# RWKV stage of a four-stage network: from strings of a whole sequence to strings of one chunk

## The chip, the cores and the metric

The kernel runs on one core of a Trainium2 chip. The metric is the device time of one execution in microseconds (us). Three runs of the kernel before gave 1712.28, 1715.19 and 1717.48 us; the median is 1715.19 us.

The core has a matrix engine (PE; its weight loads are shown apart as PEld), a vector engine (DVE), an activation engine (ACT), a general engine (POOL) and a queue that issues transfers (SP). Each works through its own queue in order; they wait for each other by semaphores.

## The reference

Four stages work on an input of 4 sequences, 1024 tokens and 128 channels: an RWKV block, a mixture of experts with grouped routing, a linear attention with decay, and a causal attention with a second mixture of experts. Only the first is touched. Its time mixing, cut to what matters:

```python
def step(carry, kv):              # over the tokens
    aa, bb = carry
    kk, vv = kv
    p = jnp.maximum(bb, u + kk)
    e1 = jnp.exp(bb - p)
    e2 = jnp.exp(u + kk - p)
    out = (e1 * aa + e2 * vv) / (e1 + e2)
    p2 = jnp.maximum(bb, kk)
    e1b = jnp.exp(bb - p2)
    e2b = jnp.exp(kk - p2)
    return ((e1b * aa + e2b * vv, p2 + jnp.log(e1b + e2b)), out)
```

Around it stand a layer norm, a shift by one token, three projections (k, v, r) and a sigmoid gate. Channel mixing follows on the sum: a layer norm, a shift by one token that takes its first token from the end of the sequence, a projection to 512 channels with a squared relu, one back to 128, and a gate.

## The kernel before

The activations stay on the chip with the channels on the 128 partitions and the tokens along the free dimension. A sequence of 1024 tokens is two chunks of 512 (`CH`, `NH`); an instruction of the stage works on 128x512 float32 numbers. The recurrence over the tokens is three scans of the vector engine per chunk: a running maximum (`mx`, L262), a running sum (`ss`, L273) and the weighted values (`aa`, L289). What a scan leaves at the end of chunk 0 is copied into `carry` (`keep`, L211) and read at the start of chunk 1 (`chained`, L206).

The stages are called A (RWKV), B (experts), C (linear attention) and the attention loop. A, B and stage C of sequences 0 and 1 are placed on the engines by the tile framework's scheduler, which goes by program order as a priority and by what is ready, and so lets stages overlap. The attention loop behind them is written out by hand, with stage C of sequences 2 and 3 inside it.

Stage A is a generator (`stage_a`, L186). A sequence is one string of work: time mixing of chunk 0 (L221 to L311), time mixing of chunk 1, then channel mixing of both (L315 to L346). Each `yield` ends a step; a loop (L721 to L730) takes one step of every running sequence per round. It holds at most three sequences (`SIDE = 3`) and starts a new one when twelve rounds have passed since the last start (`BEHIND = 12`) and fewer than three run:

```python
if waiting and (len(running) == 0 or (len(running) < SIDE and count >= BEHIND)):
    b = waiting.pop(0)
    running.append(stage_a(b, rooms_a[b % SIDE]))
    count = 0
running = [g for g in running if not next(g, True)]
```

Buffers go by sequence: `own` is `_0`, `_1` or `_2`, and under it there is one each of the nine chunk buffers `hs`, `xxx`, `k`, `v`, `r`, `mx`, `d`, `ss` and `aa`, one each of `x1` and `h2` (a whole sequence), and two of the scratch `rs` (`Room.scratch`, L111). So the two chunks of a sequence share one set. All three sequences take their matmul results from three PSUM banks (`pp_a`), with time mixing and channel mixing on the same three. Two more banks (`pp_c`) belong to stage C and later stages, three (`pp_b`) to stage B.

The lines that the prediction goes by: L227 to L234 load, centre and transpose a chunk (`x_t`); L242 to L252 the norm and the token shift (`xxx`); L255 the projection to `k`; L310 the last instruction of a chunk's time mixing (`h`); L345 the last of a chunk's channel mixing (it adds to `xT`). In stage B, L463 opens each of a sequence's 18 units (9 groups of experts in each of two halves), L482 and L483 close a half. In stage C, L526 is the first instruction of a half. Stage C's buffer pool `pc` is opened on the left side of the on-chip memory, where `pa`, the pool of stage A, has been closed just before.

Of the kernel before, what the change touches and what calls it, by code (L numbers as in the profile page):

```python
# [18 lines left out]
P = 128  # L19
NB = 4  # L20
# [19 lines left out]
def sandwich(ctx: ExitStack, tc: tile.TileContext, x, vecs, cmats, rope, wa, wb, wc, wd, out):  # L40
# [61 lines left out]
    class Room:  # L102


        def __init__(self, pool, stage, bufs, sbuf=None, own=""):
            self.pool, self.stage, self.bufs, self.sbuf, self.own = pool, stage, bufs, sbuf, own
# [4 lines left out]
        def scratch(self, tag, shape=(P, CH), bufs=2):  # L111
            return self.sbuf.tile(list(shape), FP, tag=tag + self.own, name=tag, bufs=bufs)
# [73 lines left out]
    def stage_a(b, pp):  # L186

        own = pp.own
        ts = vec("time_shift")

        def buf(tag, shape=(P, CH), bufs=1):
            return pa.tile(list(shape), FP, tag=tag + own, name=tag, bufs=bufs)

        x1 = buf("x1", (P, T))
        h2 = buf("h2", (P, T + 1))

        carry = buf("carry", (P, 4), 2)
        nc.gpsimd.tensor_copy(carry[:, 0:1], ts)
        nc.gpsimd.memset(carry[:, 1:2], 0.0)
        nc.gpsimd.memset(carry[:, 2:3], 1.0)  # L200
        nc.gpsimd.memset(carry[:, 3:4], 0.0)

        def chained(tag, which):

            t = buf(tag, (P, CH + 1))
            nc.gpsimd.tensor_copy(t[:, 0:1], carry[:, which : which + 1])  # L206
            return t

        def keep(t, which, h):
            if h + 1 < NH:  # L210
                nc.gpsimd.tensor_copy(carry[:, which : which + 1], t[:, CH : CH + 1])  # L211

        def sigmoid_steps(dst, src, plus=0.0):
            nc.vector.tensor_scalar(dst, src, plus, -41.0, ALU.add, ALU.max)
            yield
            nc.scalar.activation(dst, dst, AF.Exp, scale=-1.0)
            nc.scalar.activation(dst, dst, AF.Ln, bias=one)
            nc.scalar.activation(dst, dst, AF.Exp, scale=-1.0)
            yield

        for h in range(NH):  # L221
            c = chunk(h)
            if (b, h) not in xtok:
                load_x(b, h)
            xt = xtok[b, h]
            at = means[:, b, h * 4 : h * 4 + 4]
            nc.vector.tensor_reduce(at, xt, AX.X, ALU.add)  # L227
            nc.vector.tensor_scalar_mul(at, at, 1.0 / P)
            nc.gpsimd.tensor_sub(xt, xt, at.unsqueeze(2).to_broadcast([P, 4, P]))
            yield  # L230
            pt = pp([P, CH], "x_t")
            for j in range(4):
                nc.tensor.transpose(pt[:, j * P : (j + 1) * P], xt[:, j, :], ident)
            nc.scalar.copy(xT[b][:, c], pt)  # L234
            yield

            var = mean_square(pp, xT[b][:, c])
            yield
            rs = rstd(var, eps5, to=pp.scratch("rs"))
            both = rstd(var, eps10, scale=1.0 + 1e-5)  # L240
            yield
            nc.gpsimd.tensor_mul(x1[:, c], xT[b][:, c], rs)  # L242
            hs = chained("hs", 0)
            nc.vector.scalar_tensor_tensor(
                hs[:, 1:], xT[b][:, c], vec("ln1_w"), both, op0=ALU.mult, op1=ALU.mult
            )
            nc.vector.tensor_scalar_add(hs[:, 1:], hs[:, 1:], vec("ln1_b"))
            keep(hs, 0, h)
            yield
            xxx = buf("xxx")  # L250
            nc.gpsimd.tensor_sub(xxx, hs[:, 1:], hs[:, :CH])
            nc.vector.scalar_tensor_tensor(xxx, xxx, ts, hs[:, 1:], op0=ALU.mult, op1=ALU.add)  # L252
            yield
            k, v, r = buf("k"), buf("v"), buf("r")
            nc.scalar.copy(k, project(pp, wat[:, 0, :], xxx, "k_ps"))  # L255
            nc.vector.tensor_copy(v, project(pp, wat[:, 1, :], xxx, "v_ps"))
            yield
            later_r = sigmoid_steps(r, project(pp, wat[:, 2, :], xxx, "r_ps"))


            mx = chained("mx", 1)
            nc.vector.tensor_tensor_scan(mx[:, 1:], k, k, mx[:, 0:1], op0=ALU.max, op1=ALU.max)  # L262
            keep(mx, 1, h)
            yield
            next(later_r)
            d = buf("d")
            nc.gpsimd.tensor_sub(d, mx[:, :CH], mx[:, 1:])
            nc.scalar.activation(d, d, AF.Exp)
            ss = chained("ss", 2)
            nc.gpsimd.tensor_sub(ss[:, 1:], k, mx[:, 1:])  # L270
            nc.scalar.activation(ss[:, 1:], ss[:, 1:], AF.Exp)
            yield
            nc.vector.tensor_tensor_scan(ss[:, 1:], d, ss[:, 1:], ss[:, 0:1], op0=ALU.mult, op1=ALU.add)  # L273
            keep(ss, 2, h)
            yield from later_r
            nc.scalar.activation(d, ss[:, :CH], AF.Ln)
            yield
            nc.vector.tensor_add(d, d, mx[:, :CH])
            nc.vector.tensor_sub(d, d, k)
            yield  # L280
            e1, e2 = mx[:, :CH], k
            nc.vector.tensor_scalar_min(e1, d, 0.0)
            nc.scalar.activation(e1, e1, AF.Exp)
            nc.vector.tensor_scalar_max(e2, d, 0.0)
            nc.scalar.activation(e2, e2, AF.Exp, scale=-1.0)
            yield
            nc.vector.tensor_mul(e2, e2, v)
            aa = chained("aa", 3)
            nc.vector.tensor_tensor_scan(aa[:, 1:], e1, e2, aa[:, 0:1], op0=ALU.mult, op1=ALU.add)  # L289
            keep(aa, 3, h)  # L290
            yield

            yield from sigmoid_steps(d, d, nfirst)
            o = xxx
            nc.gpsimd.tensor_sub(o, aa[:, :CH], v)
            nc.vector.tensor_mul(o, o, d)
            yield
            nc.gpsimd.tensor_add(o, o, v)
            nc.vector.tensor_mul(o, o, r)
            yield  # L300
            nc.gpsimd.tensor_add(x1[:, c], x1[:, c], o)
            yield
            pc_ = project(pp, center, x1[:, c], "ln_c")
            var = mean_square(pp, pc_)
            yield
            rs = rstd(var, eps5, to=pp.scratch("rs"))
            yield
            now = h2[:, 1 + h * CH : 1 + (h + 1) * CH]
            nc.vector.scalar_tensor_tensor(now, pc_, vec("ln2_w"), rs, op0=ALU.mult, op1=ALU.mult)
            nc.vector.tensor_scalar_add(now, now, vec("ln2_b"))  # L310
            yield  # L311


        nc.gpsimd.tensor_copy(h2[:, 0:1], h2[:, T : T + 1])
        for h in range(NH):  # L315
            c = chunk(h)
            now = h2[:, 1 + h * CH : 1 + (h + 1) * CH]
            xx2 = buf("xxx")
            nc.gpsimd.tensor_sub(xx2, h2[:, c], now)
            nc.vector.scalar_tensor_tensor(xx2, xx2, ts, now, op0=ALU.mult, op1=ALU.add)  # L320
            yield
            rc = buf("r")
            later_r = sigmoid_steps(rc, project(pp, wat[:, 11, :], xx2, "rc_ps"))
            next(later_r)
            kcs = []
            for j in range(4):
                kc = pa.tile([P, CH], FP, tag="kc", name="kc", bufs=4)
                nc.scalar.activation(kc, project(pp, wat[:, 3 + j, :], xx2, "kc_ps"), AF.Relu)
                nc.scalar.activation(kc, kc, AF.Square)
                kcs.append(kc)  # L330
            pv = pp([P, CH], "vv_ps")
            for j in range(4):
                nc.tensor.matmul(pv, lhsT=wat[:, 7 + j, :], rhs=kcs[j], start=(j == 0), stop=(j == 3))
            yield
            yield from later_r
            nc.vector.tensor_mul(rc, pv, rc)
            nc.gpsimd.tensor_add(rc, rc, x1[:, c])
            yield
            pc_ = project(pp, center, rc, "ln_c")
            var = mean_square(pp, pc_)  # L340
            yield
            rs = rstd(var, eps5, to=pp.scratch("rs"))
            yield
            nc.vector.tensor_mul(rc, pc_, rs)
            nc.gpsimd.tensor_add(xT[b][:, c], xT[b][:, c], rc)  # L345
            yield  # L346
# [372 lines left out]
    rooms_a = [Room(pp_a, "a", 3, pa, f"_{i}") for i in range(SIDE)]  # L719
    room_b = Room(pp_b, "b", 3, pb)  # L720

    running, waiting = [], list(range(NB))
    count = 0
    while running or waiting:
        if waiting and (len(running) == 0 or (len(running) < SIDE and count >= BEHIND)):
# [553 lines left out]
```

## Time and profile before

| what | value |
|---|---|
| median of three runs | 1715.19 us |
| the profiled execution | 1715.55 us, its span 1713.8 us |
| instructions in the span | 15167 |
| granted PE clock, mean | 0.85 |
| L234, copy of a transposed chunk (8 of them) | 8.5 to 239.0 us |
| L310, end of time mixing (8 of them) | 59.0 to 279.8 us |
| L345, end of channel mixing (8 of them) | 142.9 to 317.9 us |
| L463, opening of an expert unit (72 of them) | 204.5 to 697.1 us |
| L882, first kind of work of the attention loop | from 735.3 us |

The profile is one execution. Times are from the start of its span. A row of instructions gives line, engine, operation, "what it writes <- what it reads", and either start and length in us (the timeline) or the number, the mean and the idle time ahead (the groups). What stands in brackets is the time for which the engine was idle before it, and who released it.

### The profile page before, as it was taken

The page shows a single profiled execution, that of the slowest core. Times are in us where ns is not written, and L with a number is a line of the kernel's source. Part 1 is how long each engine was busy: PE and PEld are TensorE (multiplying, and loading weights), DVE is VectorE, ACT ScalarE, POOL GpSimd, SP SyncE. Part 2 cuts the span into 40 slices and gives each one's busy share as a digit, 9 for nine tenths or more (in the row PEclk, how much of TensorE's full clock was granted, in tenths as well). Part 3 has the DMA queues.
Part 4 walks back from the last instruction along what each step waited for, and adds up shares of the span by engine and source line. Part 5 has one row for each costly group of instructions (what it writes and reads, how often), then busy time and mean ns, then how long its engine had stood idle before and what let it go on. Part 6 is the DMA issues. An engine that isn't in the chain of part 4 may idle for free.

```text
span 1713.8 us, 15167 instructions
## 1 busy us (share of the span) xinstructions
PE 1310.6 (76%) x4593; PEld 463.3 (27%) x4604; DVE 1168.9 (68%) x1991; ACT 856.7 (50%) x1565; POOL 655.9 (38%) x663
## 2 busy tenths in 40 slices
PE   2547887867865889678779869888887879889864
PEld 1213333312221323133223223322232223233311
DVE  4575676698775877867995597777779825577601
ACT  3457776624453457234436625645553345645561
POOL 5554353524252324323433363427227333122212
PEclk8669998978887999877779869987898669989996
DMA  2000110313033122101112111231113011110101
GB/s 97 13 7 6 25 50 25 96 40 108 13 111 110 53 65 85 44 12 34 45 58 70 53 57 54 70 92 46 38 37 101 21 48 64 45 61 29 54 22 56
DMA packets 59330, 90.49 MB, mean 53 GB/s; under 512 B 9904, under 2 KB 26800, under 8 KB 58544
## 3 DMA queue, kind: packets, MB, share of 16 engines
q1 hardware_dynamic: 59248, 89.52, 17.3%
q8 instruction: 36, 0.59, 0.1%
q14 instruction: 46, 0.38, 0.1%
HBM read 76.38 MB, written 12.71 MB: 52 GB/s over the span
## 4 chain that ended last, share of the span: by engine, by line
PE 32%; DVE 18%; ACT 6%; issue 4%; POOL 4%; DMA 2%; SPq 0%; POOLq 0%; DVEq 0%; ACTq 0%
PE av L937 8%; PE sc L945 5%; DVE ms L882 4%; DVE st L620 4%; ACT pr L950 3%; PE sm L874 3%; DVE ms L887 3%; PE y L1074 3%; PE sm L886 2%; PE ln_v L138 2%; PE num_ps L674 1%; POOL hid L473 1%; POOL share L1062 1%; PE sm L878 1%; PE g_ps L138 1%
## 5 line engine op out<-in xcount | busy, mean ns | idle before, releaser
L950 ACT ACTIVATE pr<-sc 128x512 f32<-128x512 f32 x576 | 328.2, 595 | 361.7 <-PE sc L945 358.0
L882 DVE TENSOR_REDUCE ms<-sm 128x1 f32<-128x512 f32 (+3 forms) x352 | 210.5, 633 | 114.2 <-PE sm L878 103.0
L945 PE MATMUL sc<-qr,keys_r 75*128 75x512 bf16 x576 | 234.1, 422 | 37.7 <-ACT pr L950 28.7
L887 DVE TENSOR_REDUCE ms<-sm 128x1 f32<-128x512 f32 x256 | 165.0, 682 | 56.4 <-PE sm L886 55.9
L937 PE MATMUL av<-pr,va 128*32 128x512 f32 x1152 | 183.1, 710 | 0.0
L954 POOL TENSOR_SCALAR_AFFINE_SELECT pr<-pr 128x512 f32<-128x512 f32 x128 | 89.4, 712 | 244.5 <-ACT pr L950 236.2
L874 PE MATMUL sm<-keys_r,qr 72*128 72x512 bf16 (+3 forms) x512 | 138.2, 337 | 46.3 <-DVE ms L882 43.9
L138 PE MATMUL ln_v<-rs,cm 128*128 128x512 f32 x176 | 113.0, 733 | 43.0 <-ACT rs L126 28.3
L473 POOL TENSOR_TENSOR hid<-hid,gate 128x512 f32<-128x512 f32 x64 | 81.9, 1280 | 162.9 <-DVE hid L468 124.6
L614 POOL TENSOR_TENSOR kv<-vrep,phi 128x512 f32<-128x512 f32 x64 | 85.6, 1342 | 115.0 <-issue 47.9
L1062 POOL TENSOR_TENSOR share<-n,every 128x512 f32<-128x512 f32 x64 | 87.2, 1373 | 91.1 <-DMA every<-row 70.5
L455 PE MATMUL y_ps<-hid,wbt 128*128 128x512 f32 x144 | 84.1, 669 | 46.3 <-DVE hid L474 44.4
L886 PE MATMUL sm<-keys_r,qr 72*128 72x512 bf16 x256 | 99.6, 417 | 25.0 <-DVE ms L887 20.6
L945 PEld LDWEIGHTS <-keys_r 75*128 75x128 bf16 x576 | 58.7, 106 | 153.2 <-issue 126.3
L878 PE MATMUL sm<-later,identb 128*128 128x128 bf16 (+2 forms) x341 | 90.5, 265 | 0.0
L474 DVE TENSOR_TENSOR hid<-hid,g 128x512 f32<-128x512 f32 x72 | 57.7, 801 | 46.7 <-POOL hid L473 39.9
L138 PE MATMUL u_ps<-n,wbt 128*128 128x512 f32 x144 | 77.3, 618 | 7.6 <-DVE hid L468 5.1
L138 PE MATMUL g_ps<-n,wbt 128*128 128x512 f32 x144 | 78.8, 630 | 3.7 <-DVE hid L463 1.6
L1074 PE MATMUL y<-share,wexp 128*128 128x512 f32 x128 | 70.8, 644 | 9.6 <-POOL share L1062 9.4
L874 PEld LDWEIGHTS <-qr 72*128 72x128 bf16 x512 | 51.0, 107 | 99.4 <-issue 82.8
L465 ACT ACTIVATE g<-hid 128x512 f32<-128x512 f32 x72 | 45.1, 626 | 55.4 <-DVE hid L463 55.3
L674 PE MATMUL num_ps<-st,cm 128*32 128x512 f32 x128 | 52.5, 777 | 25.7 <-DVE st L637 25.5
(300 smaller groups left out, 2394.9 us busy)
## 6 DMA issues: line engine op xcount, KB each, us to landing
gate<-rows SPq DMA_DIRECT2D x64, 256.0 KB
vrep<-v_rows SPq DMA_DIRECT2D x64, 256.0 KB
every<-row SPq DMA_DIRECT2D x64, 256.0 KB
qr<-dq SPq DMA_DIRECT2D x72, 128.0 KB
turn<-in_rope_dram SPq DMA_DIRECT2D x8, 512.0 KB
dq<-qp SPq DMA_DIRECT2D x8, 384.0 KB
keys_r<-dk SPq DMA_DIRECT2D x72, 32.0 KB
sums<-av_sb SPq DMA_DIRECT2D x128, 18.0 KB
```

Source lines behind the costliest of these rows:

```text
L138: nc.tensor.matmul(ps, lhsT=lhsT, rhs=rhs, start=True, stop=True)
L473: nc.gpsimd.tensor_mul(a, a, gate)
L874: nc.tensor.matmul(view[:, k, :], lhsT=qr[0:KROWS, h, tb], rhs=kr[0:KROWS, half, h // 4, 0:n_s], start=(k == 0), stop=False, skip_group_ch ...
L878: nc.tensor.matmul(view[:, :, n_s - P :], lhsT=identb, rhs=later[:, :in_bank, :], start=False, stop=True, skip_group_check=True,)
L882: nc.vector.tensor_reduce(ms[:, 0, h0 : h0 + in_bank], view, AX.X, ALU.max)
L886: nc.tensor.matmul(sc, lhsT=qr[0:KROWS, h, tb], rhs=kr[0:KROWS, 0, h // 4, :], start=True, stop=True)
L887: nc.vector.tensor_reduce(ms[:, 1, h : h + 1], sc, AX.X, ALU.max)
L937: nc.tensor.matmul(pavs[b, i][32 * g : 32 * g + 32, :], lhsT=va[:, j, g, :], rhs=pr, start=(j == 0), stop=(j == i),)
L945: nc.tensor.matmul(sc, lhsT=kr[0:ROWS, j // 4, g, j % 4 * P : (j % 4 + 1) * P], rhs=qr[0:ROWS, 4 * g : 4 * g + 4, tb], start=True, stop=True,)
L950: nc.scalar.activation(pr, sc, AF.Exp)
L1062: nc.gpsimd.tensor_mul(shares[-1], n4, gates[len(shares) - 1])
L1074: nc.tensor.matmul(y, lhsT=wexp[:, e, :], rhs=shares[e], start=False, stop=(e == 7))
```

## The change

The string of a sequence is cut into strings of a chunk. `time_mixing(b, h, pp)` is the old loop body for one chunk, `channel_mixing(b, h, pp)` the old second loop's body for one chunk; the instructions inside are the same.

- The nine chunk buffers go by chunk: chunk number `2b + h` takes set `(2b + h) % 4` (`SETS = 4`). `x1`, `h2` and `carry` go by sequence, three of each (`SEQS = 3`).
- The loop starts a chunk's time mixing six rounds after the last one's start (`BEHIND = 6`) if fewer than four run; sequence 3 waits until both channel mixings of sequence 0 are done.
- When both chunks of a sequence have had their time mixing, their channel mixings are put into a second list, from which one is started every four rounds (`BEHIND_MIX = 4`).
- Channel mixing takes its matmul results from the two banks of `pp_c`, with its own buffers `xx2` and `rc` (two each) and its own scratch (two). Time mixing keeps the three banks of `pp_a` and has four scratch buffers.
- The load of a chunk's input is issued in the second step of the chunk two places ahead of it, not by the sequence when it gets there.

```diff
-        def scratch(self, tag, shape=(P, CH), bufs=2):
-            return self.sbuf.tile(list(shape), FP, tag=tag + self.own, name=tag, bufs=bufs)
+        def scratch(self, tag, shape=(P, CH)):
+            return self.sbuf.tile(list(shape), FP, tag=tag + self.own, name=tag, bufs=self.kept)
...
-    def stage_a(b, pp):
...
-        x1 = buf("x1", (P, T))
-        h2 = buf("h2", (P, T + 1))
-        carry = buf("carry", (P, 4), 2)
...
+    SETS, SEQS = 4, 3
...
+    def time_mixing(b, h, pp):
+        own = f"_{(NH * b + h) % SETS}"
...
+        if h == 0:
+            x1, h2, carry = (
+                pa.tile([P, n], FP, tag=f"{tag}_{b % SEQS}", name=tag, bufs=1)
+                for tag, n in (("x1", T), ("h2", T + 1), ("carry", 4))
+            )
+            of_sequence[b] = x1, h2, carry
...
+        xt = xtok.pop((b, h))
...
         nc.scalar.copy(xT[b][:, c], pt)
+        if NH * b + h + 2 < NB * NH:
+            load_x(*divmod(NH * b + h + 2, NH))
         yield
...
+    def channel_mixing(b, h, pp):
+        x1, h2, _ = of_sequence[b]
+        if h == 0:
+            nc.gpsimd.tensor_copy(h2[:, 0:1], h2[:, T : T + 1])
...
-            xx2 = buf("xxx")
+        xx2 = pa.tile([P, CH], FP, tag="xx2", name="xx2", bufs=2)
...
-            rc = buf("r")
+        rc = pa.tile([P, CH], FP, tag="rc", name="rc", bufs=2)
...
-    SIDE, BEHIND = 3, 12
-    rooms_a = [Room(pp_a, "a", 3, pa, f"_{i}") for i in range(SIDE)]
+    rooms_a = Room(pp_a, "a", 3, pa, 4), Room(pp_c, "c", 2, pa, 2, "m")
...
+    BEHIND, BEHIND_MIX = 6, 4
+    running, behind_a = [], []
+    done = set()
+    coming_a = [(b, h) for b in range(NB) for h in range(NH)]
+    count = count_mix = BEHIND
+    while running or behind_a or coming_a:
+        if coming_a and count >= BEHIND:
+            b, h = coming_a[0]
+            free = sum(kind == "time" for kind, *_ in running) < SETS
+            if free and (b < SEQS or {("mix", b - SEQS, k) for k in range(NH)} <= done):
+                running.append(("time", b, h, time_mixing(b, h, rooms_a[0])))
+                coming_a.pop(0)
+                count = 0
+        for item in list(running):
+            kind, b, h, steps = item
+            if next(steps, True):
+                running.remove(item)
+                done.add((kind, b, h))
+                if kind == "time" and {("time", b, k) for k in range(NH)} <= done:
+                    behind_a += [("mix", b, k, channel_mixing(b, k, rooms_a[1])) for k in range(NH)]
+        if behind_a and count_mix >= BEHIND_MIX:
+            running.append(behind_a.pop(0))
+            count_mix = 0
+        count_mix += 1
+        count += 1
```

## The prediction

> **What bounds the kernel now.** I read the engine shares and the forty slices of the page first, to see whether one engine is full anywhere.
>
> ```profile
> PE 1310.6 (76%) x4593; PEld 463.3 (27%) x4604; DVE 1168.9 (68%) x1991; ACT 856.7 (50%) x1565; POOL 655.9 (38%) x663
> ...
> PE   2547887867865889678779869888887879889864
> ```
>
> No engine is full over the span, and the first three slices of PE (43 us each) read 2, 5, 4. That is where the change works: the line views put the RWKV stage between 5 and 319 us and the attention loop behind 735 us. So I asked for busy time per stretch. I cut the stretches where a chunk's time mixing ends (the starts of L310 in the timeline: 59, 94, 123, 128, 161, 199, 237 and 280 us). Columns: length, then busy us and count of PE, weight loads, DVE, ACT, POOL, then clock and DMA.
>
> ```profile
> 5.00:59.00 54.00, 19.81 (x33) 7.79 (x33) 25.48 (x43) 18.61 (x33) 27.09 (x61) 0.75 0.17 63
> 59.00:128.00 69.00, 32.51 (x49) 11.84 (x50) 48.34 (x66) 38.67 (x69) 38.58 (x41) 0.67 0.04 12
> 128.00:199.00 71.00, 56.03 (x142) 22.98 (x141) 41.95 (x85) 51.83 (x95) 28.57 (x27) 0.98 0.01 4
> 199.00:237.00 38.00, 32.98 (x77) 13.26 (x75) 25.25 (x34) 31.63 (x59) 20.00 (x21) 1.00 0.25 54
> 237.00:280.00 43.00, 31.59 (x67) 11.99 (x65) 31.72 (x43) 29.64 (x51) 18.68 (x15) 0.88 0.09 32
> 280.00:319.00 39.00, 36.31 (x99) 16.09 (x100) 26.19 (x64) 25.94 (x47) 13.47 (x12) 1.00 0.19 53
> ```
>
> In the first 54 us nothing is half busy except POOL, which is there by a hair: this is a chain of short instructions handed from engine to engine. The waits of 20 to 120 us say the same:
>
> ```profile
> PE k_ps L138 <- DVE xxx L252: 41.2, 5, 12.5
> ACT k L255 <- PE k_ps L138: 29.6, 4, 9.6
> ...
> PE ln_v L138 <- ACT rs L126: 19.9, 7, 4.8
> ACT d L268 <- POOL d L267: 16.7, 5, 5.9
> ```
>
> Each engine waits for its neighbour in the chain, not for a full queue. Then the stage's end:
>
> ```profile
> 272.69 1.27 POOL L483 TENSOR_TENSOR xT<-xT,rs 128x512 f32<-128x512 f32 x1 [0.34 <-DVE rs L482]
> ...
> 317.52 0.62 ACT L526 ACTIVATE rs<-xT 128x512 f32<-128x512 f32 x1
> 317.90 0.69 DVE L474 TENSOR_TENSOR hid<-hid,g 128x512 f32<-128x512 f32 x1
> 317.91 1.82 POOL L345 TENSOR_TENSOR xT<-xT,r 128x512 f32<-128x512 f32 x1
> ```
>
> L483 finishes the first half of sequence 0 for the linear attention at 274 us, yet its first instruction (L526) starts at 317.5, beside the RWKV stage's last one (L345): the pool of the linear attention lies where the RWKV pool lay. So the **end of the RWKV stage** gates stage C of sequence 0, and the expert stage B(0), which ends at 339 us (L482 at 338.0, L483 behind it), gates the rest. Between 339 and 735 us DVE is 308.8 of 396 busy and PE 294.4: that is dense, and I take it to move as a block.
>
> **The change, part by part.** No arithmetic is added or removed; each instruction of the stage is there eight times (or four) as before.
>
> *Order.* Counting the yields of the code, time mixing has 22 steps and channel mixing 7. Before, a sequence is one string of 22+22+7+7 steps, a new one starts 12 rounds after the last, and at most three run: 118 rounds, 47 with one item running, 24 with two, 47 with three. After, a chunk starts every six rounds, and channel mixing is a string of its own: 82 rounds, 19, 11, 14, 27, 9 and 2 of them with one to six items. Sequence 3 waits for sequence 0's mixing either way, but its two chunks then run six rounds apart instead of one behind the other.
>
> What is a round worth? The stretches above are known numbers of rounds: 22 with one or two items in 54 us (2.45 each), 24 with mostly three in 69 (2.9), 22 with three in 71 (3.2), 22 with one in 43 (1.95). A line through these, 1.6 us and 0.5 us per item, gives 47x2.1+24x2.6+47x3.1 = 307 us for the 314 measured. After: 82x1.6 + 0.5x248 items = 255 us, so the stage ends near 260 instead of 319 us: **-58 us**. Sequence 0's mixing ends in round 40, near 139 us instead of 167 (L345, second start 165.6): **-28 us**. More than three items at once the trace does not show. Bounds of such an item-round: nothing below (engines with room absorb it), 1.9 us above (the PE time of a mixing step, 22 matmuls of 0.6 us in 7 rounds). There are 27+18+6 = 51 item-rounds beyond the third; at nothing the stage takes 230 us, at 1.9 it takes 326. I stay at 0.5, the slope of the rows, since no engine would be full: the stage's and B(0)'s work up to 339 us is DVE 209.6, PE 227.7, ACT 208.2 us, which by 306 us is 0.74 of PE at most, as in the dense stretch.
>
> *Stage B(0).* Its 18 units (starts of L463) run from 204 to 323 us: 7 us apart beside two RWKV sequences, 4 us when it has PE to itself. It begins 40 us behind the mixing of sequence 0, so near 179; some 11.5 units fit up to 260, the other 6.5 take 29 us, and the tail behind the last unit is 17 us (322.7 to 339 now): 306 instead of 339, **-33 us**.
>
> *Sum.* Stage C's gate moves by 58 us, the expert stage by 33; behind them both are mixed on DVE and PE, so I take the mean: **-45 us**. The profiled span 1713.8 gives 1669; the median of the runs shown is 1.4 us above that span (the profiled run itself 1.75), so **1670 us**.
>
> *Four sets of nine chunk buffers, three of x1, h2 and carry.* These carry the overlap above and cost no instruction. Chunk 1's scans wait for chunk 0's carries, a new wait at six rounds' distance: the hs carry is copied at 19.3 us, mx at 25.4, ss at 29.7, aa at 38.4, each within 32 us of the chunk's first instruction, and the second chunk needs each of them 13 us later than the first did. Nothing waits, provided POOL is not late; if it is, the scan heads DVE's queue and the other chunks' DVE work stands behind it, one scan's worth (1.3 us) per carry.
>
> *Input loads.* Still eight on SP's queue (0.43 us to issue), each two chunks ahead. DVE waits for them 4.6 us in all now; a chunk now frees its input buffer in its second round, so I book nothing, at worst two landings of 2 us.
>
> *Channel mixing on the two linear attention banks, scratch of 4 and 2.* Time mixing gets three banks alone. I book nothing: the mean square of one mixing chunk needs both banks for about 5 us, the next one's first projection stands behind it in PE's queue, and that is priced as a rival below.
>
> *A rule against it.* On DVE, mean minus median of the two-input instructions is 0.22 (L252), 0.21 (L262), 0.04 (L273), 0.11 (L278), 0.29 (L279) and 0.19 us (L289): 1.04 us a chunk, 8 us in all, with POOL 56% busy between 59 and 128 us. The Trainium skill (SBUF — State Buffer, Who interferes with whom) says that a VectorE instruction with two SBUF inputs and a GpSimd one reading SBUF lock each other out for a whole instruction. Taken at its word, each of nine such instructions meets a running POOL one (1.25 us) with chance 0.56 and waits half of it: 3.2 us a chunk, 25 us in all, and the change, which packs them closer, would keep only -28. I take the row, raised with POOL's share to 0.7: +2 us, within the rounding. That the medians (1285 ns, 692 ns) stay clean at 56% speaks for the row.
>
> **Rivals.**
>
> *The gain is swallowed by stage B.* If B(0) crawls at 10 us a unit beside four chunks (8 units by 260 us), the other 10 take 45 and the tail 17: 322, -17 us, 1698. For it: the RWKV stage is traced first, so B gets what is left. Against: C's gate still moves, and the room from 5 to 59 us is real.
>
> *More gain.* If items beyond the third cost nothing and PE's clock (0.67 from 59 to 128 us) rises with its load, the stage takes 230 us and B(0) starts near 125: -75 us, 1640.
>
> *Slower: a matmul at the head of PE's queue waits for a bank.* Six rounds apart, one chunk's x_t, the next's r_ps and an older one's ln_c and ln_v ask for four of three banks, five times in the stage; and mixing chunks four rounds apart meet on two banks four times. An ln_c bank is held 9.2 us (49.5 to 58.7) in time mixing, 6.3 us (311.6 to 317.8) in channel mixing. If every meeting costs its whole hold, that is 5x9.2+4x6.3 = 71 us against the 58 won: stage end 332, +13 us, 1728. It decides only above 58/71, four fifths of every hold. Against: other matmuls run in that time now, and banks come free one by one.
>
> That the order written is not the order run is contained in the second rival: the scheduler orders by priority and readiness, but the chunk ends follow the rounds, so the order in the code does count.
>
> **How the numbers follow.** Forecast (-20 to -75 us) 62%, more gain 8%, swallowed (0 to -20) 16%, slower 14%. A measurement of this kernel tells 0.3% (5 us) from no change. Of the swallowed case 10 points are beyond 5 us, so faster 0.80, same 0.06, slower 0.14. The range leaves out the slower case and the far half of the larger gain: 1635 to 1713. The likeliest case alone is 1640 to 1695.
>
> **What would show it.** Time mixing's last L310 near 230 us instead of 280, the stage's last channel-mixing instruction near 260, stage C's first within a few us of it, B(0)'s end near 306, the attention loop's first near 690 and the length behind that unchanged at 979 us within 5. PE and DVE should be above half busy from 30 us on, with a higher clock. Wrong would be: rounds longer than 3.8 us, PE waiting with an idle queue for a bank's reader, or an unchanged start of the attention loop.

## The result, and the profile after

The changed kernel takes 1724.62 us (median), the kernel before 1718.6 us in the same session; the ratio is 1.0036, with an interval of 1.002 to 1.0051. It is slower by some 6 us where 45 us less was forecast. The profiled execution is further off than the medians: its span is 1726.2 us, 12.4 us above the 1713.8 of before. All of this lies ahead of the attention loop, which starts at 747.8 us instead of 735.3; what lies behind its start takes 978.5 us in both.

The page's shares and PE's forty slices (43 us each), after the change:

```profile
PE 1330.1 (77%) x4593; PEld 470.2 (27%) x4604; DVE 1176.0 (68%) x1991; ACT 857.9 (50%) x1565; POOL 661.6 (38%) x663
...
PE   3367888777775879678679878888877778899964
```

The first three slices read 3, 3, 6 instead of 2, 5, 4, one tenth more in sum: PE gets to work hardly sooner. The stage did get shorter. These are the lines of the timeline (start, length) that answer to the stage's end shown before. L354 is now the last instruction of channel mixing, L491 and L492 close a half of B(0), L535 is stage C's first:

```profile
290.37 1.28 POOL L354 TENSOR_TENSOR xT<-xT,rc 128x512 f32<-128x512 f32 x1
...
310.69 0.68 DVE L491 TENSOR_TENSOR rs<-y_ps,rs 128x512 f32<-128x512 f32 x1
311.45 1.27 POOL L492 TENSOR_TENSOR xT<-xT,rs 128x512 f32<-128x512 f32 x1 [5.41 <-DVE rs L491]
312.76 0.62 ACT L535 ACTIVATE rs<-xT 128x512 f32<-128x512 f32 x1
...
375.07 1.26 POOL L492 TENSOR_TENSOR xT<-xT,rs 128x512 f32<-128x512 f32 x1 [2.68 <-DVE rs L491]
```

The RWKV stage ends at 292 us, 28 earlier than before. But stage C now starts behind L492, the first half of B(0), which ends at 313 instead of 274; and B(0) as a whole ends at 376 instead of 340. The last gate is another one now: the expert stage of sequence 0, which had time to spare before, ends last. Its first unit (L472, formerly L463) starts at 249 us, 45 later than before, though sequence 0's channel mixing ended nine earlier (157.6 against 166.9). Where those 92 us went is seen in the gate computation, a chain of small instructions ahead of the units:

```profile
179.46 0.68 DVE L391 TENSOR_TENSOR n<-xT,ln_v 128x512 f32<-128x512 f32 x1
...
196.16 0.29 DVE L400 TENSOR_SCALAR s<-gate_ps 128x128 f32<-128x128 f32 x1 [2.82 <-PE gate_ps L395]
...
199.75 0.31 ACT L401 ACTIVATE s<-s 128x128 f32<-128x128 f32 x1
...
209.33 0.21 DVE L402 TENSOR_SCALAR s<-s 128x128 f32<-128x128 f32 x1
...
223.21 1.35 DVE L435 TENSOR_TENSOR masked<-s,allowed 128x128 f32<-128x128 f32 x1
...
237.08 0.29 DVE L438 TENSOR_TENSOR sel<-sel,s 128x128 f32<-128x128 f32 x1
```

The first and the last of these in the kernel before:

```profile
176.81 0.68 DVE L382 TENSOR_TENSOR n<-xT,ln_v 128x512 f32<-128x512 f32 x1
...
191.01 0.29 DVE L429 TENSOR_TENSOR sel<-sel,s 128x128 f32<-128x128 f32 x1
```

Each takes 0.2 to 1.4 us, and between L401 and L402, say, lie 9.3 us in which DVE's queue holds RWKV instructions. From L391 to L438 it is 58 us, before it was 14. DVE is busy for 48.9 of the 70 us from 179 to 249; for the rest it mostly waits for the input of an RWKV instruction. L409, for one, has had its own input since 210.5, but DVE stands 1.55 us at a `v` that waits for PE (212.08), and L409 runs at 215.55.

### The profile page after: what moved, and what is told of

Its sections match the earlier page's. It is cut to its first block, busy times and chain, and to the rows that moved or that the text cites. A ratio compares the mean times of both kernels' runs of the same rounds, so it can differ in the third digit from the quotient of the medians.

```text
span 1726.2 us, 15146 instructions
## 1 busy us (share of the span) xinstructions
PE 1330.1 (77%) x4593; PEld 470.2 (27%) x4604; DVE 1176.0 (68%) x1991; ACT 857.9 (50%) x1565; POOL 661.6 (38%) x663
## 4 chain that ended last, share of the span: by engine, by line
PE 33%; DVE 17%; ACT 6%; issue 4%; POOL 4%; DMA 1%; SPq 0%; POOLq 0%; DVEq 0%; ACTq 0%
PE av L962 8%; PE sc L970 5%; DVE ms L907 4%; DVE st L629 3%; PE sm L899 3%; ACT pr L975 3%; PE y L1099 3%; PE sm L911 3%; PE ln_v L138 2%; DVE ms L912 2%; POOL hid L482 1%; PE num_ps L683 1%; POOL share L1087 1%; PE sm L903 1%; DMA vrep<-v_rows 1%
## 5 line engine op out<-in xcount | busy, mean ns | idle before, releaser
L899 PE MATMUL sm<-keys_r,qr 72*128 72x512 bf16 (+3 forms) x512 | 142.2, 345 | 46.2 <-DVE ms L907 43.9
L483 DVE TENSOR_TENSOR hid<-hid,g 128x512 f32<-128x512 f32 x72 | 61.2, 852 | 50.1 <-POOL hid L482 43.4
```

The costliest lines, as they stand in the source:

```text
L899: nc.tensor.matmul(view[:, k, :], lhsT=qr[0:KROWS, h, tb], rhs=kr[0:KROWS, half, h // 4, 0:n_s], start=(k == 0), stop=False, skip_group_ch ...
```

## The experiments

Three readings stood at the start. Theory S: B(0) sets the end now, since its gates starve behind the RWKV work, which comes first in the code. Theory R: the RWKV stage itself sets the end. And the two banks that channel mixing moved to may be the fault. Each run was timed against the kernel before. The table has the places in the profiles that the text goes by, in us, each from one profiled execution; executions of the kernel before lay between 1704 and 1729 us in one session, so a few us between two places prove little. The columns: the end of sequence 0's channel mixing, the first expert unit, the ends of B(0)'s first half and of B(0), the end of the RWKV stage, the start of the attention loop.

| kernel | mix 0 | unit | B(0) h0 | B(0) | RWKV | loop | ratio to before |
|---|---|---|---|---|---|---|---|
| before | 166.9 | 204.5 | 274.0 | 340.1 | 319.7 | 735.3 | |
| after | 157.6 | 249.3 | 312.7 | 376.3 | 291.6 | 747.8 | 1.0036 (1.002 to 1.0051) |
| gates early | 158.4 | 198.8 | 291.6 | 359.6 | 292.9 | 730.5 | 0.9937 (0.9912 to 0.9962) |
| before, gates early | 167.6 | 197.2 | 277.2 | 353.2 | 337.7 | 754.1 | 1.0059 (1.0037 to 1.0081) |
| nine rounds | 133.5 | 181.2 | 283.3 | 351.7 | 293.1 | 722.4 | 0.9905 (0.988 to 0.9931) |
| mixing on three banks | 164.8 | 205.2 | 302.9 | 371.1 | 304.1 | 742.1 | 0.9974 (0.9951 to 0.9996) |
| four rounds | 152.5 | 236.4 | 299.9 | 362.5 | 278.8 | 734.0 | 0.9977 (0.9949 to 1.0004) |
| nine rounds, gates early | 132.1 | 172.8 | 283.0 | 353.1 | 304.2 | 730.7 | 0.9943 (0.9919 to 0.9967) |
| twelve rounds | 132.5 | 170.9 | 284.3 | 348.2 | 326.9 | 743.7 | 1.0029 (1.0007 to 1.005) |
| before, mixing on two banks | 165.5 | 228.5 | 294.8 | 365.6 | 319.2 | 745.9 | 1.0017 (0.9992 to 1.0043) |
| seven rounds | 132.4 | 226.3 | 290.9 | 354.4 | 269.8 | 725.8 | 0.9912 (0.9886 to 0.9938) |
| seven rounds, gates early | 132.8 | 181.2 | 277.8 | 345.4 | 279.0 | 716.2 | 0.9861 (0.9819 to 0.9903) |
| transposes on two banks | 155.5 | 226.7 | 301.3 | 364.2 | 285.5 | 733.8 | 0.9959 (0.9938 to 0.9981) |
| nine, transposes on two banks | 123.9 | 185.4 | 283.5 | 352.2 | 293.3 | 726.5 | 0.99 (0.9864 to 0.9936) |

One relation runs through it: the loop starts at the later of (RWKV end + 416.5) and (B(0) end + 371). The two constants were read off the first six rows, each of which it fits to 1 us. Of the eight rows that came later it fits five within 1.5 us, and in three the loop is later, by 3 (the last row), 7 (nine rounds with gates early) and 9 us (before, mixing on two banks). In the latter two both candidates fall within 4 us of each other. What lies behind the loop's start took 974 to 985 us in all these profiles and is not counted in it.

**Gates early.** In the changed kernel, and likewise in the kernel before, the gates of sequence 0 are given a place in the RWKV loop instead of behind it:

```diff
                 done.add((kind, b, h))
+                if kind == "mix" and b == 0 and {("mix", 0, k) for k in range(NH)} <= done:
+                    running.append(("gates", 0, 0, gates_b(0, room_b)))
...
-    whole(gates_b(0, room_b))
```

Expected in the changed kernel:

> Theory S (stage B of sequence 0 is what ends the stretch before the attention loop, and after the change its gate computation starves behind the RWKV work of higher priority: from its norm at 179 us to its first transposed gates at 246, against 177 to 202 before): putting the gates into the RWKV loop right behind sequence 0's channel mixing gives them their place in the queues, so the first gates come near 205, the first expert unit near 210 instead of 249, and the attention loop starts some 15 to 25 us earlier than in the changed kernel (748): 723 to 733, the time 10 to 25 us below the changed kernel. Theory R (the RWKV stage itself, eight chunks in file through three banks, sets the end): gates moved up only push RWKV work back, the attention loop starts within 5 us of 748.

Expected in the kernel before:

> The same edit on the kernel before. Theory S: there the gates took only 25 us, so little is to be had: the attention loop starts at 730 to 736 (735 now), the time within 5 us of before. Theory R: also no change. A gain here as large as in the changed kernel would say that the edit helps for a reason of its own and is no evidence on the change.

In the changed kernel the first unit came at 199 instead of 249 and the loop at 730.5, as S had it; the time fell below that of before. In the kernel before the same edit made things worse. S missed there: it overlooked that before, the RWKV stage was the later gate. The edit pushed that stage's end from 320 to 338 and the loop from 735 to 754, by 18 and 19 us. So here the edit paid where B(0) was the last and cost where the RWKV stage was. This pair is the clearest evidence that the change moved the bound from one to the other.

**Distance of the chunks.** Only the constant is changed:

```diff
-    BEHIND, BEHIND_MIX = 6, 4
+    BEHIND, BEHIND_MIX = 9, 4
```

> The changed kernel with chunks nine rounds apart in place of six. Theory S: less RWKV work of higher priority beside the gates of sequence 0, which take nearer to 30 than 67 us; the attention loop starts 5 to 12 us earlier than 748. Theory R: the stage needs 103 rounds in place of 82 and ends later, the attention loop starts later than 748 by 5 to 20 us.

Four rounds in its place:

> The changed kernel with chunks four rounds apart. So far every run fits: attention loop starts at the later of (end of the RWKV stage + 417) and (end of B of sequence 0 + 372). Theory S: the stage's end stays near 292 (the chunks go in file, 24 us each, whatever the distance), but sequence 0 has to share with more chunks, its mixing ends later than 157 and B(0) later than 375: start of the loop 750 to 765, time 0 to 15 us above the changed kernel. Theory F (the file comes from the distance of six, which puts a chunk's transposes right behind the last one's r projection in PE's queue): at four they come ahead of the k projection, the file shortens below 20 us a chunk, the stage ends before 280 us.

Twelve:

> Twelve rounds apart. If the distance of six only made chunks wait in file, twelve costs the stage no more than 120 rounds of 2.6 us: end near 310, B(0) near 340, loop from 727 (310 + 417): time 5 us above the run with nine rounds and still below before. If nine gained by chance of the placement, anything from 720 to 760 is possible.

And nine together with the early gates:

> Nine rounds apart and the gates in the RWKV loop. Theory S: both bring B(0) forward; alone they ended it at 350 and 358, together near 335; the RWKV stage ends near 293 as in both. Loop from 335 + 372 = 707 or 293 + 417 = 710, the later: 710, time 10 to 14 us below the run with nine rounds alone.

Nine rounds beat both kernels, by more than S had said: sequence 0's mixing ended at 133.5 instead of 157.6, while the stage ended where it did with six (293 against 292). The 16 rounds more (98 by a count of the code; the expectation's 103 was a miscount) cost nothing. Twelve missed its number: the stage ended at 327, not 310, and was the last again. Four missed too: loop at 734 where 750 or later was expected. Sequence 0's mixing at 152.5 and the gates' slowness (first unit 84 us behind it) are as bad as with six, but the stage ended at 279, the one hit of Theory F; its file did not fall below 20 us a chunk (k projections 24.8 to 194.0, 24.2 us apart). Nine with early gates missed by 20 us: the gates came 8 us sooner, the RWKV stage 11 us later, B(0) ended no sooner (353). Its time rose with that (0.9943 against 0.9905), where 10 to 14 us less was expected. So the distance does not act by being large or small, and the gates' place is not worth the same everywhere.

**Seven rounds.** The timeline of PE in the changed kernel shows why six is a special number:

```profile
51.77 2.07 PE L138 MATMUL ln_v<-rs,cm 128*128 128x512 f32 x2 [6.32 <-ACT rs L126]
60.96 2.07 PE L138 MATMUL k_ps<-xxx,wat 128*128 128x512 f32 x2 [7.11 <-DVE xxx L258]
62.83 1.92 PE L138 MATMUL v_ps<-xxx,wat 128*128 128x512 f32 x2
64.53 1.42 PE L138 MATMUL ln_c<-x,cm 128*128 128x512 f32 x2
71.86 2.07 PE L138 MATMUL ln_v<-rs,cm 128*128 128x512 f32 x2 [5.91 <-ACT rs L126]
```

The ln_c of 64.5 us is the first chunk's. Its input (L307) was there at 47.5, but ahead of it in PE's queue stand the third chunk's ln_v, which waits 6.3 us, and its k projection, which waits 7.1 us, both for their own inputs and with PE idle. A chunk started twelve rounds later does its k and v in round 18, the first chunk its ln_c in round 19. At seven rounds the third chunk starts 14 rounds later and its k comes in round 20.

```diff
-    BEHIND, BEHIND_MIX = 6, 4
+    BEHIND, BEHIND_MIX = 7, 4
```

> Chunks seven rounds apart, one more than in the changed kernel. In the changed kernel's trace the first chunk's ln_c matmul is ready at 47 us but stands in PE's queue behind the third chunk's k projection (step 7 of a chunk started 12 rounds later, ahead of step 20 of the first), which waits for its input until 61: the chunk's time mixing ends at 77 instead of 57 to 59 us. Theory H (that place in the queue is what makes sequence 0 late): at seven the k projection comes behind ln_c; the first chunk ends at 57 to 62, sequence 0's mixing near 135 instead of 157, and with it the first expert unit comes well before 249 (190 to 225), B(0) ends near 355, the loop starts near 726. Theory C (closeness itself, more chunks sharing the engines, makes it late): seven lies a third of the way from six to nine, the first chunk ends near 70, the mixing near 149, the loop starts near 740.

PE's timeline of that kernel:

```profile
51.06 2.08 PE L138 MATMUL ln_v<-rs,cm 128*128 128x512 f32 x2 [6.70 <-ACT rs L126]
52.93 1.91 PE L138 MATMUL ln_c<-x,cm 128*128 128x512 f32 x2
56.01 2.08 PE L138 MATMUL ln_v<-rs,cm 128*128 128x512 f32 x2 [1.17 <-ACT rs L126]
60.24 2.07 PE L138 MATMUL k_ps<-xxx,wat 128*128 128x512 f32 x2 [2.15 <-DVE xxx L258]
```

ln_c now runs at 53, and the k projection behind it is no later than it was. One round of distance brought sequence 0's mixing from 157.6 to 132.4 (Theory H: 135, C: 149) and the loop to 725.8 (H: 726, C: 740), and the stage ended 22 us sooner besides. Two numbers were off: the first chunk ended at 65, not 57 to 62, and the first unit at 226, just past 225; the gates still took their time. The first chunk ended 13 us sooner (65.1 against 77.8). That is half of the 25 us of the mixing; the rest was not traced to single instructions.

The order is only half of it. Where the distance divides twelve, some chunk starts twelve rounds behind the first (as the second sequence does in the kernel before), and its k projection stands ahead of the first one's ln_c. In the kernel before, and at twelve rounds, that did no harm: the k projection had its input early, at 46 and 47 us, and the first chunk ended at 59 and 60. At four rounds it was later still than at six. PE's timeline of before, then of the kernel with four rounds:

```profile
46.03 2.07 PE L138 MATMUL k_ps<-xxx,wat 128*128 128x512 f32 x2 [12.49 <-DVE xxx L252]
47.90 1.77 PE L138 MATMUL v_ps<-xxx,wat 128*128 128x512 f32 x2
49.50 1.02 PE L138 MATMUL ln_c<-x,cm 128*128 128x512 f32 x2
...
73.31 2.07 PE L138 MATMUL k_ps<-xxx,wat 128*128 128x512 f32 x2 [13.42 <-DVE xxx L258]
75.18 1.91 PE L138 MATMUL v_ps<-xxx,wat 128*128 128x512 f32 x2
76.88 1.91 PE L138 MATMUL ln_c<-x,cm 128*128 128x512 f32 x2
```

At four rounds ln_c had its input at 50.5 and ran at 76.9, and the first chunk ended at 90. So ready work is held up where it stands behind work whose input is late.

> Seven rounds apart and the gates in the RWKV loop. With Theory H sequence 0's mixing ends near 135, the first expert unit comes near 180, but the first half of B(0) has not ended before 274 us in any run, whenever it started, and B(0) follows 66 us behind it: B(0) ends at 340 to 352, the RWKV stage near 300, the loop starts at 712 to 723. Against the run with nine rounds alone (722) a gain of at most 10 us.

With the gates early as well, the first unit came at 181, B(0) ended at 345 and the loop started at 716.2: 1691.0 us (the median of six executions), ratio 0.9861 (0.9819 to 0.9903) to before. The RWKV stage ended at 279 where 300 was expected. This has the lowest ratio found, and is faster than both kernels; its interval overlaps those of seven and of nine rounds alone.

The first unit now starts within 2 us of the 179 that the prediction had, yet B(0) ends at 345 and not at 306. These are its first and tenth unit and its end:

```profile
181.19 0.68 DVE L472 TENSOR_SCALAR hid<-g_ps 128x512 f32<-128x512 f32 x1
...
275.12 0.69 DVE L472 TENSOR_SCALAR hid<-g_ps 128x512 f32<-128x512 f32 x1 [5.29 <-PE g_ps L138]
...
344.14 1.26 POOL L492 TENSOR_TENSOR xT<-xT,rs 128x512 f32<-128x512 f32 x1 [1.99 <-DVE rs L491]
```

The first nine units took 10.4 us each beside the RWKV stage. With nine rounds alone it was 10.7, with the gates early at six 10.0.

**The banks.** Channel mixing back on time mixing's three banks, and the reverse, the move to two banks alone in the kernel before:

```diff
-    rooms_a = Room(pp_a, "a", 3, pa, 4), Room(pp_c, "c", 2, pa, 2, "m")
+    rooms_a = Room(pp_a, "a", 3, pa, 4), Room(pp_a, "a", 3, pa, 2, "m")
```

> The changed kernel with channel mixing back on time mixing's three banks, one part of the change undone. If the two banks of the linear attention are the cause (a mixing chunk's centred result and its variance take both, and PE's queue waits behind them), the time falls back to before's or below. Theory S and R: 15 matmul results of a mixing chunk now go in file with time mixing through three banks, the RWKV stage ends later than 292 us, the time is equal or up to 15 us above the changed kernel.

```diff
+            pp = Room(pp_c, "c", 2, pa, own)
             later_r = sigmoid_steps(rc, project(pp, wat[:, 11, :], xx2, "rc_ps"))
```

> The kernel before with one part of the change alone: channel mixing on the linear attention's two banks. The stage is then three sequences on three banks for time mixing only. If the banks matter, the RWKV stage ends 5 to 15 us before 319 and the loop starts as much before 735 (it is the stage's end + 417 there). If not, no change within 4 us.

Undone in the changed kernel, the stage ended 12 us later and yet the loop started 6 us earlier, and the time fell to before's, as forecast if the two banks were at fault. The first unit came 44 us sooner; B(0)'s end gained only 5 us of that, since its first nine units then took 10.6 us each instead of 6.8. Alone in the kernel before, the RWKV stage ended at 319.2, as it had (319.7), the first unit came 24 us later and the loop 11 in the profiled execution, which neither forecast had; the time (1.0017, 0.9992 to 1.0043) can't be told from before. So this part gave the RWKV stage nothing when alone, and in both profiles the gates came later with it. That mixing with banks of its own runs ahead of the gates on the other engines fits, but was only argued. The other parts of the change (the buffer sets, the scratch, the earlier loads) were not undone one by one.

**The file of chunks.** The k projections of the changed kernel (by the copies behind them) follow each other at 17.7, 21.4, 27.7, 24.7, 26.1, 38.5 and 30.2 us. Each chunk's transposes stand behind the last one's r projection. Were they waiting for a bank of the three?

```diff
-        pt = pp([P, CH], "x_t")
+        pt = rooms_a[1]([P, CH], "x_t")
```

> The changed kernel with the transposes of time mixing on the linear attention's two banks. Theory F2 (chunks go in file, 24 to 27 us each, because a chunk's transposes get a bank only behind the last chunk's k, v and r, since the three banks go round in the order of the code): the second chunk's transposes come near 12 instead of 29 us, the file shortens to 20 us a chunk or less, the RWKV stage ends before 275. Theory P (the file is the length of the chain from norm to r projection, or the engines' work): transposes early, but the k projections keep their distance, the stage ends at 285 to 295. The loop's start follows B(0), which neither makes certain: 735 to 748.

> Nine rounds apart with the transposes on the linear attention's banks, as a candidate for a better kernel. F2: stage end 280 or less (293 with nine alone), B(0) 5 to 10 us earlier than 352, loop from 712 to 717. P: within 4 us of the run with nine rounds alone, loop from 718 to 726.

The second chunk's transposes did move, from 28.8 to 11.5 us, and the k projections did not (41.0 instead of 41.7, the last 209.8 instead of 210.4): Theory P. The stage ended at 285.5, the loop started at 734, just below what was expected. The kernel still gained: its ratio to before is 0.9959, against 1.0036 for the change, with the first unit 23 us sooner; what brought that was not traced. With nine rounds it gave nothing (loop at 726.5, half a microsecond outside P's range). The run with seven rounds bears on the file too: with the same work and the same chain, its last k projection comes at 182.0 instead of 210.4. So neither the chain's length nor the engines' work sets the file of six rounds as a floor; the order in the queues adds to it.

## Why the prediction was wrong, point by point

**What bounds the kernel: right.** The first 54 us are a chain, and the RWKV stage's end gated stage C before. The run with early gates in the kernel before confirms it: stage end and loop moved by 18 and 19 us.

**The stage's end, -58 us: right in direction, half in size.** It came out at -28. The term that was mis-sized is the round, 1.6 us + 0.5 us per item: 82 rounds took (292-5)/82 = 3.5 us each instead of 3.1. More than three items at once is not what cost it. By a count of the code, four, seven, nine and twelve rounds' distance give 78, 84, 98 and 119 rounds and the same 248 items, so the formula has the stage end at 254, 263, 286 and 319. Measured were 279, 270, 293 and 327. It is 7 to 8 us short at seven, nine and twelve, but 25 at four and 32 at six, though seven has 45 item-rounds beyond the third and six has 51. Four and six are also the two at which ready work was seen behind a late k projection. So what the formula lacks is most likely the order in the queues; only the first chunk's part of it was traced.

**Sequence 0's mixing, -28 us: -9.** The round count supposed that a round passes for all chunks alike. In fact each engine's queue is in order, and a ready ln_c stood 17 us behind another chunk's norm and k projection. Seven rounds show it: one round apart, 25 us, and the mixing ended at 132, ahead of the forecast's 139.

**Stage B(0), -33 us: +36.** This is the step that failed, in two terms. The first is "It begins 40 us behind the mixing of sequence 0": measured were 92. I took the 38 us of the trace of before as the length of the gate computation, but it was a length beside one or two RWKV items. The early gates brought the 92 back to 40. The second is the pace of the units, 7 us beside the RWKV stage. That from first unit to end it was 127 us as forecast was luck: B(0) began so late that only three units came before 260 us, not 11.5. Where it began near the forecast's 179, it took 164 us (seven rounds with early gates) and 171 us (nine rounds), at 10 us and more a unit, and ended at 345 and 352. In none of the runs did it end before 340, where 306 was forecast. The 4 us of a unit with PE to itself was no measured case either: in the trace of before the last eight gaps between units are 6.4 us in the mean, and the RWKV stage ran beside all but the last unit (the sum itself goes on with 4.5).

**The sum as a mean of two gates.** The later one counts, not the mean. Before, B(0) had 24 us to spare (340 + 371 = 711 against 735). It slipped by 36 and ate the reserve; what was over is the 12 us of the span. I had shown both gates, and did not ask which of them was last and by how much.

**Costs booked at nothing.** Channel mixing on two banks: 6 us of the loop's start in the changed kernel and, in one profile whose excess the medians do not show, 11 alone. The POOL and DVE lock: for time mixing the row was right and the rule's reading as 17 us more was not; its nine two-input means of before add up to 9.10 us a chunk, those of after to 9.12. Channel mixing's token shift (L320, now L329) was not counted: it went from 0.75 to 1.38 us in the mean, 5 us over its eight.

**Rivals.** The slower rival had a matmul at the head of PE's queue wait for a bank and hold up those behind; the matmul was there, but it waited for its input. The swallowed rival had B(0) crawl at 10 us a unit. In the changed kernel it crawled in its gates and ended at 376 instead of the rival's 322; once the gates came early, it did crawl at that pace.

## What to carry to other kernels

When work of several strings is interleaved in a fixed order, write down which instruction of one string stands right ahead of which of another in each in-order queue; a distance that differs by one step can decide whether ready work waits behind unready work, and the one ahead does harm only if its input is late. Packing a high-priority stage closer takes room from the low-priority chain behind it, so ask what that chain has in reserve before it becomes the bound, and take its length beside the new load, not from the old trace. Where two chains gate a common point, forecast each and take the later.

## What the hardware showed that was not expected

In time mixing's sum POOL and DVE got no more in each other's way, but single DVE instructions did. These are three lines of the changed kernel, two of POOL and one of DVE's gate chain, in the timeline:

```profile
222.77 1.64 POOL L346 TENSOR_TENSOR rc<-rc,x 128x512 f32<-128x512 f32 x1 [4.96 <-DVE rc L345]
...
233.98 1.64 POOL L354 TENSOR_TENSOR xT<-xT,rc 128x512 f32<-128x512 f32 x1 [4.34 <-DVE rc L353]
...
234.42 1.35 DVE L162 TENSOR_TENSOR eq<-eq,nth 128x128 f32<-128x128 f32 x1
```

L162 takes 0.29 us in the kernel before. Here it starts 0.44 us into a POOL instruction and ends at 235.77, 0.15 us behind the end of it (235.62); L435, shown above, likewise ends at 224.56 behind POOL's 224.41. That is the lock of whole instructions that the Trainium skill (SBUF — State Buffer, Who interferes with whom) describes for two SBUF inputs. On a 0.29 us instruction it shows as a factor of nearly five. In the gate chain of before two instructions were drawn out like this (L422 to 1.05 us, L180 to 1.14), in that of after six, some 6 us of its 58. In time mixing's sum it does not show, but channel mixing's token shift is drawn out too. The first line is of before, the others are of the changed kernel:

```profile
202.61 0.75 DVE L320 SCALAR_TENSOR_TENSOR xxx<-xxx,vt,h 128x512 f32<-128x512 f32 x1 [2.77 <-POOL xxx L319]
...
197.96 2.04 POOL L328 TENSOR_TENSOR xx<-h 128x512 f32<-128x512 f32 x2
199.03 3.18 DVE L329 SCALAR_TENSOR_TENSOR xx<-xx,vt,h 128x512 f32<-128x512 f32 x2 [0.80 <-POOL xx L328]
```

Before, POOL was idle during all eight of these. In the changed kernel POOL shifts the second chunk of a sequence right behind the first, and six of the eight meet a POOL instruction and take 1.51 to 1.76 us.

PE's granted clock was low where the gates starved: 0.78, where it had read 0.98 and 1.00 between 128 and 237 us before. The windows of the changed kernel (length, busy us and count of PE, weight loads, DVE, ACT, POOL, then clock and DMA) from the mixing's end to the gates' first norm pair, and on to the first unit:

```profile
157.00:179.00 22.00, 18.14 (x31) 6.98 (x30) 12.04 (x16) 15.52 (x28) 9.65 (x10) 0.77 0.00 0
179.00:249.00 70.00, 55.41 (x118) 21.81 (x117) 48.85 (x84) 45.71 (x83) 27.64 (x29) 0.78 0.01 2
```

PE reads 79% busy in the second, at a clock of 0.78: part of that is pairs of passes that take 2.07 us (the k projection at 208 us) instead of 1.02 (the ln_c at 219). So a high share of busy PE there is no sign of a full engine. Whether the low clock held the gates up or came of the waiting, no run here separates.
